# A four-layer graph network on one core: y of layer 2 by rows, layer 1's degrees a batch ahead, and a batch of layer 3 that ends in halves

## The chip, the core and the metric

The kernel runs on one core of a Trainium2 chip. The metric is the device time of one execution in microseconds (us), lower is better. A core has five engines that run side by side, each with a queue of its own: TensorE (PE; its weight loads are listed as PEld), VectorE (DVE), ScalarE (ACT), GpSimd (POOL) and SyncE (SP). SP and POOL issue the transfers (DMAs) here; the data is moved by 16 DMA engines that all queues share. TensorE writes its results to PSUM, all other data on the core lies in SBUF.

## The reference

Sixteen graphs (B = 16) of 1024 nodes (N) with 128 features (D = 128) go through four layers; after each, x is replaced by a layernorm of x + layer(x).

```python
x = _layernorm(x + _L0_gnn_ref(x, adj, ...), axis=-1)            # attention, gated
x = _layernorm(x + _L1_gnn_ref(x, adj, nodemask, ...), axis=-1)  # three SAGE steps
x = _layernorm(x + _L2_gnn_ref(x, adj, ...), axis=-1)            # attention, three gates
x = _layernorm(x + _L3_gnn_ref(x, adj, ...), axis=-1)            # three graph convolutions
```

Layer 1 first thins out the adjacency matrix row by row, then runs three SAGE steps on the thinned matrix, and joins their results by one linear map:

```python
deg = jnp.clip(jnp.sum(adj, axis=-1, keepdims=True), 1.0, None)
agg = jnp.einsum('bij,bjd->bid', adj, x) / deg
out = agg @ Wr + x @ Wx + b
nrm = jnp.maximum(jnp.linalg.norm(out, axis=-1, keepdims=True), NORM_EPS)
return out / nrm * mf[..., None]
...
h1 = _bn(jax.nn.relu(_sage(x, adj_d, Wr1, Wx1, b1, mf)), g1, be1)     # h2, h3 likewise
xc = jnp.concatenate([h1, h2, h3], axis=-1) * mf[..., None]
return (xc @ Wl + bl) * mf[..., None]
```

Here mf is the node mask as a float. The last line is what the code calls y.

## The kernel before

`fast_kernel` runs the four layers in stages over the 16 batches. A second, general kernel stands behind a flag that is computed at the end; in these executions it is skipped. The stages, in time: layer 0 to about 610 us; the thinning to about 990 us; the three SAGE steps (`Step`, l = 0, 1, 2) to about 1636 us; layers 2 and 3 together to the end.

**Order of work.** Each batch's work in a stage is a Python generator that writes instructions and stops at each `yield`. `take_turns` (L811) resumes a list of generators one after the other until all are done. `in_rounds` (L815) does the same with due times: `yield 5` means not to be resumed for five rounds. What is written thus is a program order. From it, a planner sets at build time the order on each engine: the earliest written instruction that is ready by the planner's own estimate of durations goes next. So an instruction can stand in its queue well ahead of its written place, as a filler, where the planner saw an engine without other work. On the chip every queue is then taken in that fixed order. Tiles come from pools with a number of slots per name (`bufs`); a new tile of the name waits until an old one is released. On a queue, an instruction that waits holds all behind it.

**SAGE step 0** (L1510 to L1525). For the i-th batch in `order` (8 to 15, then 0 to 7) the list of generators is: `load` of batch i + 2 (A and x), `first` of batch i + 1, `out` of batch i, `keep` of batch i - 1. `first` (L1392) computes the degrees of its batch: 32 small matmuls of A with a block of twos (`degree_product`, L1276), four copies on ACT to a row on one partition (L1397), a transfer from there to eight partitions, issued by POOL (d<-row, L1399), a minimum, a scaling and a reciprocal on DVE (L1400 to L1403), a transfer to DRAM by POOL (L1404), and a load by SP that spreads the result over all partitions (rdeg, L1389). The next turns of `first` transpose x, split x into two halves hi and lo (L1272, L1273; lo has one slot), cast A to 32 bit (the tiles a, L1293 on DVE and L1295 on ACT), and multiply (L1306), scaled by rdeg (L1416). `keep` multiplies A with the new state in the same way. The matrices A of batches 8 to 15 are on chip; those of 0 to 7 are loaded (A<-dil_d, 1 MB each, L1369) into four slots.

**Layers 2 and 3** (L1546 to L1816). Per batch there are four generators: `before` (y, the layernorm of layer 1, the operands of the attention), `attention` (eight tiles), `mix` (the gates, layer 2's end) and `convolve` (layer 3). In one call of `in_rounds`, batch b - 2 convolves, b - 1 mixes, b attends and b + 1 is prepared; a first call prepares batches 0 and 1, and a last one ends batches 13 to 15.

In `before`, y is formed transposed. With the columns' scaling taken into Wl by `take_norms`, three matmuls per half of 512 nodes have the 128x128 matrix Wl fixed and the states hb moving (L766 for b >= 2, L1636 for b < 2, which uses a PSUM tile py of both halves). ACT adds the bias column blcol and writes yT (L1641). Eight transposes turn yT (L759), DVE multiplies by the mask (yn, L1645) and adds to x (L1648), and `normed` (L787) does the layernorm: statistics and ln_nb on DVE, the power -1/2 on POOL (ln_rstd, L745), the scaling on ACT (L801). `scaled_parts` (L1605) has in layer 3 the other form: a block of states fixed, a weight matrix moving.

`normed` takes a list of pieces; with `spans(True)` a batch is done in two halves. `convolve` does so for the last batch alone (`last`), which also stores by SP; the others store by POOL (L1799). After the stage the check flag is made on DVE (L1829 to L1834), and each engine reads it (L1842).

Of the kernel before, what the change touches and what calls it, by code (L numbers as in the profile page):

```python
# [22 lines left out]
P = 128  # L23
# [616 lines left out]
def fast_kernel(ctx: ExitStack, tc: tile.TileContext, t: dict, out: bass.AP, flag: bass.AP):  # L640
# [554 lines left out]
    class Layers23:  # L1195
# [8 lines left out]
        def weights(self, ps_h):  # L1204
            wts = self.wts
            self.Wl = wts.tile([P, 3, P], F32, name="Wl")
            nc.sync.dma_start(self.Wl, nat(t["L1_gnn_Wl"]))
            self.shift = wts.tile([P, 3, P], F32, name="shift")
            self.blcol = column(wts, t["L1_gnn_bl"], "blcol")
            self.W2T = transposed(wts, ps_h, matrix(wts, t["L2_gnn_W_w"], "l2W"), "l2WT", "h")  # L1210
            self.b2 = column(wts, t["L2_gnn_W_b"], "l2b")
            self.As2 = symmetric(wts, ps_h, matrix(wts, t["L2_gnn_A"], "l2A"), "l2As", "h")
            self.gw = wts.tile([P, 2, 32], F32, name="l2gw")
            nc.vector.memset(self.gw, 0.0)
            self.gb = wts.tile([P, 3], F32, name="l2gb")
# [17 lines left out]

        def take_norms(self, psum):

            pc = psum.tile([P, 1], F32, name="pc", tag="h")
            self.scaled(2)
            for l in range(3):
                nc.tensor.matmul(pc, self.shift[:, l, :], bn_ab[l][:, 1:2], start=(l == 0), stop=(l == 2))
            nc.vector.tensor_add(self.blcol, self.blcol, pc)  # L1240

        def load(self, s, b):
            s.hb = []
# [14 lines left out]
    with ExitStack() as ph:  # L1258
# [56 lines left out]
        class Step:  # L1315
# [73 lines left out]
                nc.sync.dma_start(st.rdeg, bass.AP(tensor=rdeg_d[b].tensor, offset=rdeg_d[b].offset,  # L1389
                                                   ap=[[0, P], [1, N]]))  # L1390

            def first(self, b):  # L1392

                st = self.batches[b]
                row = work.tile([1, N], F16, name="row", bufs=1)
                for acc, c in degree_product(st.A):
                    nc.scalar.copy(row[:, c], acc)  # L1397
                d16 = small.tile([NT, P], F16, name="d16", bufs=1)
                nc.gpsimd.dma_start(d16, row)  # L1399
                nc.vector.tensor_reduce(nodeg[:NT, b:b + 1], d16, AX.X, OP.min)  # L1400
                d8 = small.tile([NT, P], F32, name="d8", bufs=1)
                nc.vector.tensor_scalar(d8, d16, 0.5, 1.0, op0=OP.mult, op1=OP.max)
                nc.vector.reciprocal(d8, d8)  # L1403
                nc.gpsimd.dma_start(rdeg_d[b], d8)  # L1404
                self.load_rdeg(b)
                yield
                st.hT = work.tile([P, N], F32, name="hT")
                for p, c, _ in turned(ps_h, st.x):
                    nc.scalar.copy(st.hT[:, c], p)
                yield  # L1410
                parts = split(st.x)
                pieces = list(widened(st.A))
# [82 lines left out]
        for l in range(3):  # L1495
            step = Step(l, before)
            if l:
                before.norm()
                step.take_norm()
            if l == 2:  # L1500
                order = [b for pair in zip(order[:B // 2], order[B // 2:]) for b in pair]
            if l == 2:
                take_turns(left)
                left = []
            lead = 0 if l == 1 else 1
            take_turns([step.load(b) for b in order[:1 + lead]])
            if l == 0:
                take_turns([step.first(order[0])])
            outs = [step.out(b) for b in order]
            for i in range(B + lag[l]):  # L1510
                streams, left = left, []
                if i + 1 + lead < B:
                    streams.append(step.load(order[i + 1 + lead]))
                if l == 0 and i + 1 < B:
                    streams.append(step.first(order[i + 1]))
                kept = [step.keep(order[i - 1 - lag[l]])] if i > lag[l] else []
                if l == 2:
                    streams += kept
                if i < B:
                    streams.append(outs[i] if l < 2 else islice(outs[i], 2))  # L1520
                if l == 2 and i:
                    streams.append(outs[i - 1])
                if l < 2:
                    streams += kept
                take_turns(streams)  # L1525
                if l == 2 and i == 0:

                    wide_ctx.close()
                    l2 = Layers23()
                elif l == 2 and i == B - 4:  # L1530
# [15 lines left out]
    with ExitStack() as ph:  # L1546
# [4 lines left out]

        ps_w = ph.enter_context(tc.tile_pool(name="l2_pw", bufs=2, space=PSUM, reuse_waits="tile"))

        W2T, b2, As2, gw, gb, nbig, blcol, Wl = l2.W2T, l2.b2, l2.As2, l2.gw, l2.gb, l2.nbig, l2.blcol, l2.Wl
        (U0, U1, U2), (c0, c1, c2) = l2.U, l2.c
        l2.take_norms(ps_h)

# [65 lines left out]
        def before(s, b):  # L1623
# [1 line left out]
            if b:  # L1625
                l2.load(s, b)
            yield 2
            yT = wide("yT")
            if b < 2:

                p = ps_w.tile([P, N], F32, name="py", tag="w")
                cs = [slice(h * 512, (h + 1) * 512) for h in range(H2)]
                for ls in ((0, 1), (2,)):
                    for c in cs:
                        for l in ls:
                            nc.tensor.matmul(p[:, c], Wl[:, l, :], s.hb[l][:, c], start=(l == 0), stop=(l == 2))  # L1636
                turns = [(p[:, c], c) for c in cs]
            else:
                turns = products(ps_h, *((Wl[:, l, :], s.hb[l]) for l in range(3)))
            for p, c in turns:  # L1640
                nc.scalar.activation(yT[:, c], p, AF.Identity, bias=blcol)  # L1641
            yield 1
            yn = rows("yn", 1)
            for p, c, k in turned(ps_h, yT):
                nc.vector.tensor_mul(yn[:, k, :], tiles3(p), half_rows(mf[:, b * NT + k.start:b * NT + k.stop]))  # L1645

            for k in spans(b < 2):
                nc.vector.tensor_add(s.xn[:, k, :], s.xn[:, k, :], yn[:, k, :])  # L1648
            normed(small, s.xn, b < 2)
            yield 5  # L1650
            s.xT = wide("xT", 2)
            for p, c, _ in turned(ps_h, s.xn):
                nc.scalar.copy(s.xT[:, c], p)
# [92 lines left out]

        def convolve(s, b):

            last = b == B - 1
            at = Place(last)  # L1750
            diag = bass.AP(tensor=s.A8.tensor, offset=s.A8.offset, ap=[list(s.A8.ap[0]), [N + P, NT], [1, P]])
            nc.vector.tensor_tensor(diag, diag, identb[:, None, :].to_broadcast([P, NT, P]), op=OP.add, saturate=False)
# [32 lines left out]
            r = at.of("prop", at.x)  # L1785
            for piece in propagated(at, r, parts, A, dB):
                yield 1
            for k in spans(last):
                c = slice(k.start * P, k.stop * P)
                nc.scalar.activation(r[:, c], r[:, c], AF.Identity, bias=c2)  # L1790
            yield 2 if last else 5
            for p, c, k in turned(at.psum, r, at.ptag):
                nc.vector.tensor_add(s.xn[:, k, :], s.xn[:, k, :], tiles3(p))
                if last:
                    normed(small, s.xn, pieces=[k])
            if not last:
                normed(small, s.xn)
            for k in spans(last):
                (nc.sync if last else nc.gpsimd).dma_start(nat(out[b])[:, k, :], s.xn[:, k, :])  # L1799
            yield  # L1800

        state = l2.state
# [63 lines left out]
```

## Time and profile before

| what | value |
|---|---|
| median of three runs | 2682.58 us (2681.59 to 2685.39) |
| the profiled execution: its own time | 2682.24 us |
| its span, first to last instruction | 2680.4 us |
| mean granted TensorE clock | 0.982 |
| busy: PE, DVE, ACT, POOL | 2521.3, 2102.6, 1969.3, 330.8 us |
| weight loads (PEld) | 1800.2 us |
| chain that ended last, by engine | PE 52%, DVE 19%, ACT 11%, POOL 4%, DMA 3% |
| d<-row (L1399), issue to landing, min/median/max | 1.5/1.6/4.7 us |
| A<-dil_d in step 0 and 1, the same | 4.7/4.8/8.6 us |

How to read the lines of the profile. A line of a group or timeline gives the start (us from the span's start), the length, engine, line of the code, operation, the tile written and the tiles read, the shapes, and how many instructions (x) were merged. The bracket at its end says how long the engine had been idle, and what it then got. A line of the chain of waits gives start, length, engine and line: it is followed back from the last instruction, at each step to what released it. In the table of 40 slices each digit is the busy share of one slice in tenths. Matmuls overlap: the time from one to the next in a group is shorter than the length of one.

### The profile page before, as it was taken

To read this page: it belongs to the slowest core of one execution; us is meant where nothing else is said; L and a number is where in the kernel's file an instruction comes from. 1 tells how busy PE (TensorE), PEld (TensorE's weight loads), DVE (VectorE), ACT (ScalarE), POOL (GpSimd) and SP (SyncE) were. 2 spreads that over 40 slices of the span, in tenths; PEclk is the share of its full clock that TensorE was granted. 3 is DMA by queue.
4 is the path that set the end of the run, shared out by engine and by line. 5 is a ranking of instruction groups with operands and counts; after the bars stand their busy time and mean duration, and the time that the engine had idled before them with its cause. 6 is when DMAs were issued, how large, how long until landed. Compare 5 with 4: busy or idle time off the path is not lost.

```text
span 2680.4 us, 44092 instructions
## 1 busy us (share of the span) xinstructions
PE 2521.3 (94%) x16136; PEld 1800.2 (67%) x16136; DVE 2102.6 (78%) x5830; ACT 1969.3 (73%) x3172; POOL 330.8 (12%) x300
## 2 busy tenths in 40 slices
PE   7999999997889879999999998999999999999986
PEld 5667777765666658887788895466666666666655
DVE  6888888987898867777778875777878787887885
ACT  7898889886888776666555534777777777777773
POOL 0001111103000002111122232001101000001010
PEclk9999999998999989999999998999999999999998
DMA  5555545520000052233366672112221111111100
GB/s 193 181 176 171 173 161 174 179 96 21 2 3 2 1 221 90 100 111 134 133 241 236 211 283 111 40 38 73 74 91 64 64 63 63 63 63 63 48 24 26
DMA packets 109187, 285.59 MB, mean 107 GB/s; under 512 B 12192, under 2 KB 52128, under 8 KB 101792
## 3 DMA queue, kind: packets, MB, share of 16 engines
q1 hardware_dynamic: 87776, 196.58, 21.7%
q0 software_dynamic: 21184, 86.09, 8.8%
q8 instruction: 129, 2.11, 0.3%
q14 instruction: 98, 0.80, 0.1%
HBM read 202.78 MB, written 79.82 MB: 105 GB/s over the span
## 4 chain that ended last, share of the span: by engine, by line
PE 52%; DVE 19%; ACT 11%; issue 8%; POOL 4%; DMA 3%; POOLq 0%; ACTq 0%; DVEq 0%; SPq 0%
PE ph L1618 8%; PE acc L1678 7%; PE acc L1306 7%; PE ph L766 6%; PE ph L1432 4%; PE ph L759 3%; PE pmm L1690 3%; PE acc L973 2%; PE pmm L724 2%; ACT em L985 2%; PE ph L1605 2%; ACT xn L801 2%; DVE mid L1096 2%; DVE keep L1147 2%; POOL ln_rstd L745 2%
## 5 line engine op out<-in xcount | busy, mean ns | idle before, releaser
L973 PEld LDWEIGHTS acc<-hs,em 128*128 128x128 f32 x2048 | 248.7, 192 | 37.9 <-issue 26.8
L973 PE MATMUL acc<-hs,em 128*128 128x128 f32 x2048 | 269.1, 279 | 0.7 <-DVE hs L989 0.3
L1678 PE MATMUL acc<-ex,hs 128*128 128x512 f32 x512 | 248.9, 596 | 7.4 <-DVE hs L1705 4.5
L724 PE MATMUL pmm<-xT,G 128*128 128x512 f32 x512 | 251.4, 604 | 1.4 <-DVE mx L983 0.7
L801 ACT ACTIVATE xn<-xn,ln_nb,ln_rstd 128x128 f32<-128x128 f32 x512 | 204.7, 480 | 55.9 <-DVE ln_nb L799 55.8
L1306 PE MATMUL acc<-a,hi 128*128 128x512 f32 x768 | 233.6, 398 | 11.1 <-DVE a L1293 8.0
L1306 PE MATMUL acc<-a,lo 128*128 128x512 f32 x768 | 229.6, 393 | 5.8 <-DVE lo L1273 5.8
L745 POOL TENSOR_TENSOR ln_rstd<-ln_rstd,mhalf 128x8 f32<-128x8 f32 (+1 forms) x68 | 108.3, 1593 | 969.2 <-DVE ln_rstd L742 513.4
L983 DVE CUSTOM_DVE_ANT_0 em<-pmm,msk 128x1024 f32<-128x1024 f32 x128 | 155.9, 1218 | 35.1 <-PE pmm L724 32.8
L985 ACT ACTIVATE em<-em,mx 128x1024 f32<-128x1024 f32 x128 | 146.0, 1141 | 48.2 <-DVE mx L983 46.5
L1698 ACT ACTIVATE ex<-em,mn 128x1024 f32<-128x1024 f32 x128 | 146.9, 1147 | 45.0 <-DVE mn L1695 44.0
L1690 PE MATMUL pmm<-G,hT 128*128 128x512 f32 (+3 forms) x416 | 175.3, 523 | 0.1
L1695 DVE CUSTOM_DVE_ANT_0 em<-pmm,msk 128x1024 f32<-128x1024 f32 x128 | 155.4, 1214 | 24.5 <-PE pmm L1692 22.3
L1306 PEld LDWEIGHTS acc<-a,hi 128*128 128x128 f32 x768 | 142.2, 189 | 42.4 <-DVE a L1293 10.6
L1306 PEld LDWEIGHTS acc<-a,lo 128*128 128x128 f32 x768 | 143.5, 189 | 40.2 <-DVE lo L1273 10.5
L1156 ACT ACTIVATE carry<-pc,negone 128x1024 fp8e4<-128x1024 f32 x128 | 141.3, 1115 | 26.7 <-PE pc L1155 23.8
L931 ACT ACTIVATE carry<-an 128x1024 fp8e4<-128x1024 f32 x128 | 134.1, 1049 | 23.9 <-DMA an<-in_adj 23.3
L980 ACT ACTIVATE msk<-carry,l0nbig 128x1024 bf16<-128x1024 fp8e4 x128 | 145.9, 1140 | 0.0
L1686 ACT ACTIVATE msk<-A,nbig 128x1024 bf16<-128x1024 fp8e4 x128 | 144.3, 1138 | 0.0
L1618 PE MATMUL ph<-A,hi 128*128 128x512 f32 x512 | 143.2, 420 | 0.8 <-DVE zn L1607 0.6
L1678 PEld LDWEIGHTS acc<-ex,hs 128*128 128x128 f32 x512 | 88.6, 190 | 76.8 <-issue 54.7
L1295 ACT CAST a<-A 128x1024 fp32r<-128x1024 fp8e4 x96 | 98.4, 1048 | 54.5 <-PE acc L1306 53.4
(317 smaller groups left out, 6186.6 us busy)
## 6 DMA issues: line engine op xcount, KB each, us to landing
an<-in_adj SPq DMA_DIRECT2D x128, 512.0 KB, 4.1
adj_d<-carry POOLq DMA_DIRECT2D x16, 1024.0 KB, 4.6
A<-dil_d SPq DMA_DIRECT2D x16, 1024.0 KB, 5.6
rdeg<-rdeg_d SPq DMA_DIRECT2D x32, 512.0 KB, 3.8
A<-adj_d SPq DMA_DIRECT2D x16, 1024.0 KB, 4.8
ag_d<-ag POOLq DMA_DIRECT2D x24, 512.0 KB, 5.4
ag<-ag_d SPq DMA_DIRECT2D x24, 512.0 KB, 5.5
x_d<-xn POOLq DMA_DIRECT2D x16, 512.0 KB, 3.9
```

The lines of the kernel that those rows point to most:

```text
L724: nc.tensor.matmul(p[:, h * 512:(h + 1) * 512], lhsT, rhs[:, h * 512:(h + 1) * 512], start=True, stop=True)
L745: nc.gpsimd.tensor_tensor(r, r, mhalf[:, :n], op=OP.pow)
L766: nc.tensor.matmul(p, W, x[:, c], start=(i == 0), stop=(i == len(pairs) - 1))
L801: nc.scalar.activation(r[:, k.start + i, :], r[:, k.start + i, :], AF.Identity, scale=rstd[:, i:i + 1], bias=nb[:, i:i + 1])
L973: nc.tensor.matmul(s.acc[:, c], em[:, c], hs, start=(jt == 0 and k % 4 == 0), stop=(jt == NT - 1 and k % 4 == 3))
L983: nc.vector.tensor_tensor_reduce(em, e, msk, 1.0, 3.0e38, op0=OP.add, op1=OP.min, accum_out=mn)
L985: nc.scalar.activation(em, em, AF.Exp, scale=-1.0, bias=mn, accum_out=sm)
L1306: nc.tensor.matmul(acc, part[:, jt, :], pieces[h * NT // 2 + k][:, jt - 2 * k, :], start=(part is parts[0] and jt == 0), stop=(part is par ...
L1618: nc.tensor.matmul(p, part[:, jt, :], A[jt][:, c], start=(jt == 0 and i == 0), stop=(jt == NT - 1 and i == 1))
L1678: nc.tensor.matmul(s.acc[:, c], hs, ex[:, c], start=(jt == 0), stop=(jt == NT - 1))
L1690: nc.tensor.matmul(e[:, c], s.hT[:, js], s.G[:, c], start=True, stop=True)
L1695: nc.vector.tensor_tensor_reduce(row, e, msk, 1.0, 0.0, op0=OP.add, op1=OP.min, accum_out=mn)
```

## The change

Three edits, made together.

1. **y by rows.** The bias is loaded as a row over all partitions, blrow, into the slot of the raw matrix l2A (so after that one's last use); `take_norms` adds to it a 128x128 product in place of a column. In `before`, POOL multiplies mask and bias row to a tile yb (128x1024). Then for each block of 128 nodes the three states' blocks are the fixed operand and Wl the moving one, so that the sum comes out with nodes on the partitions: 24 matmuls of 128 columns in place of 6 of 512. yT, its two activations and the eight transposes are gone; DVE adds yb where it multiplied by the mask. The layernorm comes two rounds after the sums in place of one, and the next step six rounds later in place of five.
2. **Degrees a batch ahead.** The degree work is a generator of its own, `degrees`, written last in the list, for batch i + 2 in iteration i, with its product in the third turn. The load of rdeg stays in `first`. The first two batches' degrees are done ahead of the loop.
3. **Ends in halves.** Batch 14 (`near`) of layer 3 ends as batch 15 does: bias, turn, addition and layernorm by halves, stores by SP, and two rounds' pause in place of five.

```diff
-            self.blcol = column(wts, t["L1_gnn_bl"], "blcol")
...
+            self.blrow = row_bcast(wts, t["L1_gnn_bl"], P, "l2A")
...
-            pc = psum.tile([P, 1], F32, name="pc", tag="h")
+            pc = psum.tile([P, P], F32, name="pc", tag="h")
             self.scaled(2)
             for l in range(3):
-                nc.tensor.matmul(pc, self.shift[:, l, :], bn_ab[l][:, 1:2], start=(l == 0), stop=(l == 2))
-            nc.vector.tensor_add(self.blcol, self.blcol, pc)
+                nc.tensor.matmul(pc, bn_ab[l][:, 1:2].to_broadcast([P, P]), self.shift[:, l, :], start=(l == 0), stop=(l == 2))
+            nc.vector.tensor_add(self.blrow, self.blrow, pc)
...
-            def first(self, b):
+            def degrees(self, b):
 
                 st = self.batches[b]
+                yield
+                yield
                 row = work.tile([1, N], F16, name="row", bufs=1)
                 for acc, c in degree_product(st.A):
                     nc.scalar.copy(row[:, c], acc)
                 d16 = small.tile([NT, P], F16, name="d16", bufs=1)
                 nc.gpsimd.dma_start(d16, row)
+                yield
                 nc.vector.tensor_reduce(nodeg[:NT, b:b + 1], d16, AX.X, OP.min)
...
                 nc.gpsimd.dma_start(rdeg_d[b], d8)
+                yield
+
+            def first(self, b):
+
+                st = self.batches[b]
                 self.load_rdeg(b)
...
-                take_turns([step.first(order[0])])
+                take_turns([chain(step.degrees(order[0]), step.first(order[0])), step.degrees(order[1])])
...
+                if l == 0 and i + 2 < B:
+                    streams.append(step.degrees(order[i + 2]))
...
-            yT = wide("yT")
+            yb = rows("yT")
+            nc.gpsimd.tensor_tensor(yb, per_row(mf[:, b * NT:(b + 1) * NT]), per_col(blrow), op=OP.mult)
+
+            def summed(p, blocks, ls):
+                for i, j in enumerate(blocks):
+                    for l in ls:
+                        nc.tensor.matmul(p[:, i * P:(i + 1) * P], s.hb[l][:, j * P:(j + 1) * P], Wl[:, l, :],
+                                         start=(l == 0 and (i % 4 == 0 or len(ls) == 3)), stop=(l == 2 and (i % 4 == 3 or len(ls) == 3)))
+
             if b < 2:
                 p = ps_w.tile([P, N], F32, name="py", tag="w")
...
                 for ls in ((0, 1), (2,)):
...
+                    summed(p, range(NT), ls)
+                turns = [(p[:, h * 512:(h + 1) * 512], range(4 * h, 4 * h + 4)) for h in range(H2)]
             else:
-                turns = products(ps_h, *((Wl[:, l, :], s.hb[l]) for l in range(3)))
-            for p, c in turns:
-                nc.scalar.activation(yT[:, c], p, AF.Identity, bias=blcol)
-            yield 1
+                turns = ((p, blocks) for p, _, blocks in halves(ps_h))
             yn = rows("yn", 1)
-            for p, c, k in turned(ps_h, yT):
-                nc.vector.tensor_mul(yn[:, k, :], tiles3(p), half_rows(mf[:, b * NT + k.start:b * NT + k.stop]))
+            for p, blocks in turns:
+                if b >= 2:
+                    summed(p, blocks, range(3))
+                k = slice(blocks[0], blocks[-1] + 1)
+                nc.vector.tensor_add(yn[:, k, :], tiles3(p), yb[:, k, :])
+            yield 2
...
-            yield 5
+            yield 6
...
-            last = b == B - 1
+            last, near = b == B - 1, b >= B - 2
...
-            for k in spans(last):
+            for k in spans(near):
                 c = slice(k.start * P, k.stop * P)
                 nc.scalar.activation(r[:, c], r[:, c], AF.Identity, bias=c2)
-            yield 2 if last else 5
+            yield 2 if last else 2 if near else 5
...
-                if last:
+                if near:
                     normed(small, s.xn, pieces=[k])
-            if not last:
+            if not near:
                 normed(small, s.xn)
-            for k in spans(last):
-                (nc.sync if last else nc.gpsimd).dma_start(nat(out[b])[:, k, :], s.xn[:, k, :])
+            for k in spans(near):
+                (nc.sync if near else nc.gpsimd).dma_start(nat(out[b])[:, k, :], s.xn[:, k, :])
```

More of the change, by code (lines that the diff above doesn't have):

```diff
@@ L1552, in fast_kernel @@
         ps_w = ph.enter_context(tc.tile_pool(name="l2_pw", bufs=2, space=PSUM, reuse_waits="tile"))
-        W2T, b2, As2, gw, gb, nbig, blcol, Wl = l2.W2T, l2.b2, l2.As2, l2.gw, l2.gb, l2.nbig, l2.blcol, l2.Wl
+        W2T, b2, As2, gw, gb, nbig, blrow, Wl = l2.W2T, l2.b2, l2.As2, l2.gw, l2.gb, l2.nbig, l2.blrow, l2.Wl
         (U0, U1, U2), (c0, c1, c2) = l2.U, l2.c
@@ L1627, in before @@
             yield 2
-            yT = wide("yT")
+            yb = rows("yT")
[5 more added lines that the diff above has]
+                                         start=(l == 0 and (i % 4 == 0 or len(ls) == 3)), stop=(l == 2 and (i % 4 == 3 or len(ls) == 3)))
             if b < 2:
                 p = ps_w.tile([P, N], F32, name="py", tag="w")
-                cs = [slice(h * 512, (h + 1) * 512) for h in range(H2)]
                 for ls in ((0, 1), (2,)):
[L1634 to L1637, printed above, removed]
-            else:
-                turns = products(ps_h, *((Wl[:, l, :], s.hb[l]) for l in range(3)))
-            for p, c in turns:
-                nc.scalar.activation(yT[:, c], p, AF.Identity, bias=blcol)
-            yield 1
+                    summed(p, range(NT), ls)
+                turns = [(p[:, h * 512:(h + 1) * 512], range(4 * h, 4 * h + 4)) for h in range(H2)]
+            else:
+                turns = ((p, blocks) for p, _, blocks in halves(ps_h))
             yn = rows("yn", 1)
-            for p, c, k in turned(ps_h, yT):
-                nc.vector.tensor_mul(yn[:, k, :], tiles3(p), half_rows(mf[:, b * NT + k.start:b * NT + k.stop]))
+            for p, blocks in turns:
[4 more added lines that the diff above has]
+            yield 2
             for k in spans(b < 2):
```

## The prediction

> **What bounds the kernel now.** I read the busy shares in 40 slices first, then the busy time of each engine by stretches, then the chain of waits and the timeline of the three places that the change touches.
>
> ```profile
> PE   7999999997889879999999998999999999999986
> DVE  6888888987898867777778875777878787887885
> POOL 0001111103000002111122232001101000001010
> ```
>
> Each digit is a slice of 67 us. TensorE is at nine tenths wherever the change works: slices 15 to 19 (the first SAGE layer, "layer 1, step 0" in the code) and 25 to 38 (layers 2 and 3). So a microsecond counts there if it leaves TensorE's queue, or if TensorE now waits for it. The stretches are finer:
>
> ```profile
> 1083.40:1105.00 21.60, 21.39 (x145) 17.75 (x145) 16.50 (x28) 14.62 (x21) 4.29 (x5) 1.00 0.28 98
> 1264.84:1288.49 23.65, 21.82 (x147) 17.75 (x146) 16.57 (x28) 14.70 (x20) 4.20 (x5) 1.00 0.39 134
> 2320.00:2382.00 62.00, 61.69 (x269) 38.77 (x268) 49.11 (x142) 47.71 (x86) 5.95 (x4) 1.00 0.20 68
> 2600.00:2620.00 20.00, 10.85 (x31) 4.63 (x29) 15.03 (x57) 15.09 (x32) 3.93 (x3) 0.75 0.04 13
> ```
>
> The columns are length, then busy time of PE, weight loads, DVE, ACT and POOL. Row 1 is an early batch of step 0: TensorE idles 0.2 us. Row 2 is a late one: 1.8 us. Row 3 is the steady part of layers 2 and 3: TensorE idles 0.3 of 62, with 13 us to spare on DVE and 14 on ACT. Row 4 is the tail, where nothing is full.
>
> **What the Trainium skill says.** (1) "TensorE: Matmul & The Clock Gate", specification table and Part 2: the next weights load under a running matmul, and the vector engines and GpSimd take their queues strictly in order. The trace agrees: weight loads of 0.190 us (f32) stand in groups that advance every 0.111 us (L1605, 0.89 us for 8). (2) "GPSIMD Engine Reference", section 3.1: a two-input elementwise operation takes about 2.6 cycles per element, 4.5 us for 2048. For 1024 I estimate 2.2 us. The trace has no such operation. (3) "DMA: Bandwidth & Descriptors", "Issuing engines are not separate DMA queues": all transfers share 16 engines and interleave. The trace agrees: d<-row lands in 1.6 us (median), and in 4.7 us beside the 1 MB load of A.
>
> **Part 1, y by rows.** Written matmuls appear twice in the trace in f32 (168 L766 rows on hb,Wl for 14 batches, 6 written each).
>
> ```profile
> 2371.26 2.58 PE ph L766 x6
> 2373.84 0.89 PE ph L1605 x8
> ...
> 2499.71 0.44 PE ph L759 x4
> ```
>
> These are lines of the chain of waits. The first is half of the old y: 2.58 us for 6 of 512 columns, 0.43 each. The second is the form that the new y takes, a 128-column block fixed and a 128x128 matrix moving: 0.111 each. The third is half of the turn. Per batch it removes 12 x 0.43 = 5.16 and 8 x 0.11 = 0.88, and adds 48 x 0.111 = 5.34: -0.70 us of TensorE. Batches 2 to 15 lie in the full stretch: 14 x 0.70 = **-9.8**. ACT loses 2 x 0.67 us, DVE keeps its two 0.68 us reads of PSUM (an addition where it was a product): both have slack, so nothing. POOL gains the product of mask and bias. Bounds: 1.2 us (DVE's row of that size, L1648) and the estimate of 2.2, which I take; the only POOL elementwise row, a power, is far dearer (1.64 us for 8 columns). It needs only the slot of the last batch's rows, so it can run a batch early on a POOL that is busy 6 us in 62, but a layernorm's power queued behind it would wait; that is rival C. Sharing SBUF ports could slow DVE by at most those 2.2 us of its 13 spare.
>
> At the **start** of layer 2 nothing hides latency. Now the second half of batch 0 is turned behind the products of batch 1, which wait for a load (TensorE resumes at 1645.71), so its yn comes at 1650.52; batch 1's follow at 1653.04 after ACT at 1650.67 and eight transposes. In the new form, the bias row exists at about 1641.2 (blcol at 1640.92, plus 0.28), the POOL product at 1643.5, and both halves of batch 0 follow. Batch 1's sums end near 1651.0 (48 x 0.111 from 1645.71), its yn starts at once: 1.7 us before 1653.04, with batch 0's DVE work out of the way. I take **-2**, between +1 (a POOL product of twice the price) and -4. The row's load waits for the slot of l2A (last read at 1615.0, SP then idle until 1639.9): nothing.
>
> **Part 2, degrees one batch ahead.** The late batches of step 0:
>
> ```profile
> 1194.17 0.51 POOL L1399 DMA_DIRECT2D d<-row  x1 [6.55 <-ACT row L1397]
> 1198.85 0.27 DVE L1400 TENSOR_REDUCE nodeg<-d 8x1 f32<-8x128 f16 x1 [2.43 <-DMA d<-row]
> 1202.70 1.20 PE L1306 MATMUL acc<-a,hi 128*128 128x512 f32 x4 [1.30 <-DVE a L1293]
> 1207.46 0.73 PE L1281 MATMUL acc<-A,step 128*32 128x256 fp8e4 x20
> 1208.69 0.73 PE L1306 MATMUL acc<-a,lo 128*128 128x512 f32 x2 [0.50 <-DVE lo L1273]
> ```
>
> SP issues the load of A at 1193.85, the degree row leaves 0.3 us later and takes 4.7 us; DVE stands in nodeg for 2.43 us, the casts and lo queued behind it come late, and TensorE idles 1.30 and 0.50. Six batches do this (nodeg waits 14.8 us in 6 times). Groups of L1281 x20 stand at 1184.19 and 1301.83, five batches apart: 23.53 each, against 21.68 before. So 6 x 1.85 = 11.1 us is at stake. The change issues the same 32 small matmuls, 4 ACT copies (0.36 each), the POOL issue (0.51), three DVE operations (0.27, 0.20, 0.92), and the POOL store (0.50), a batch earlier and in the third turn rather than the first; on POOL this passes the hT store, the power and the ag store. By then A has landed (4.8 us after its issue), so the row should need 1.6 us again, and what is late next is TensorE itself at 21.68. The 20 matmuls at 1207.46 fill 0.65 us that TensorE would spend waiting for lo; that A is there in time (loads at 1193.85, 1217.41, one batch ahead of the written place), so I expect another batch's matmuls in the same hole. If none come: 14 x 0.65 = +9. The second product in the prologue falls where TensorE waits 2.60 us for hi; it takes 1.0 us off the path at 1003.72, and its ACT copies (1.47) may stand ahead of that hi: I set these against each other. I keep 1 us of the 11.1 for the DVE work in its new place: **-10**, between -12 and 0 (the wait goes along), or +9.
>
> **Part 3, second-to-last batch in halves.** It ends last:
>
> ```profile
> 2662.39 1.13 ACT L1790 ACTIVATE prop<-prop,c 128x1024 f32<-128x1024 f32 x1
> 2665.47 1.64 DVE L794 BATCH_NORM_STATS2 ln_st<-xn 128x6 f32<-128x128 f32 x8
> 2670.05 3.18 ACT L801 ACTIVATE xn<-xn,ln_nb,ln_rstd 128x128 f32<-128x128 f32 x8 [6.53 <-DVE ln_nb L799]
> 2673.53 0.93 POOL L1799 DMA_DIRECT2D out<-xn  x1 [3.72 <-ACT xn L801]
> ```
>
> Halved, the bias of the first half can run at about 2659.7 (its prop at 2658.72 plus 0.66), and the second half's at 2662.5, behind the last batch's normalisation on ACT. From there: bias 0.72, turn 0.7, addition 0.68, statistics 0.86 + 0.36, power 1.02 (the 4-column row), ln_nb 0.16, ACT 1.65: 2668.7 with small gaps 2669, against 2673.2. The store from SP lands in 2.2 us (last batch) against 4.6. But the check flag also ends the program: at 2671.20, then 4.0 us of a TensorE branch; it follows DVE, whose last ln_nb moves from 2669.84 to about 2667.3. So the end moves by that 2.5, not by 4.5: **-2.5**, between -1 and -5.
>
> **Sum.** -9.8 - 2 - 10 - 2.5 = -24.3. The profiled execution took 2682.24 us (span 2680.4), 0.34 below the median of three: 2657.9, so 2658.
>
> **Rivals.** A, as summed: 2658, own range 2649 to 2664. Chance 0.62. B, the degrees keep their wait or lose their hole: part 2 gives between 0 and +9 less the other 14.3, so 2668 to 2677, most of it near 2668. For it: DVE is in order, and where nodeg is put follows an estimate that knew nothing of the slow row. Against it: no large load is under way where the third turn lies. Chance 0.16. C, slower: POOL's product stands just ahead of a layernorm's power in every round. ln_nb then holds DVE's queue for up to 2.2 us, the scalings hs behind it hold TensorE (it already waits 0.29 us for hs at 2489.51). Price 14 x 2.2 = +31 on -24.3: 2689. It turns the sign from 24.3/14 = 1.7 us a round. For: three powers a round, nothing in the trace shows this product's price. Against: the product is ready a batch early. Chance 0.09. D, the new form of y doesn't pay: above 0.126 us a matmul (6.04/48) part 1 gives nothing in the steady part and the time is 2668 or more, up to 2677. For: 0.190 us weight loads. Against: L1605 at 0.111 between other work. Chance 0.08. E, gains and losses cancel, 2677 to 2688: 0.05.
>
> **Numbers.** 0.2% (5.4 us) is about what a measurement of this kernel can tell from none. Faster: A, B, D, 0.86; same: E, 0.05; slower: C, 0.09. The range from 2648 to 2672 takes all of A, most of B and part of D, about 0.8.
>
> **What would show it.** Part 1: per round of layers 2 and 3 61.63 us becomes 60.9, with no L759 on yT; POOL's product near 2.2 us. Part 2: no nodeg wait above 0.5 us, the late batches at 21.7. Part 3: out from SP near 2669. The prediction is wrong if ln_nb <- POOL grows in the rounds, if lo holds TensorE 0.8 us a batch, or if the new y advances slower than 0.12 us.

## The result, and the profile after

The kernel after takes 2660.16 us (median of 6 runs, 2656.06 to 2665.67), the kernel before 2682.09 beside it (6 runs, 2678.87 to 2685.39): a ratio of 0.9918, 95% interval 0.9906 to 0.9930, or 22 us less (19 to 25). The profiled execution took 2657.81 us, its span is 2656.1. The forecast was 2658, with a range of 2648 to 2672. The time is right; the terms that make it up are not, and the sections below are about that.

Five places can be found in both traces, each the start of one named instruction on VectorE or GpSimd. Times are us from the start of the span; the last column is what the prediction had for the stretch that ends there.

| place | before | after | ahead by | gained in the stretch | forecast |
|---|---|---|---|---|---|
| first power rn of step 0 | 1011.62 | 1012.05 | -0.4 | | |
| first power rn of step 1 (part 2 lies before it) | 1362.58 | 1346.13 | 16.5 | 16.9 | 10 |
| last power rn of step 2 | 1631.59 | 1614.67 | 16.9 | 0.5 | 0 |
| gate gt of batch 1 (the start of layer 2) | 1768.96 | 1750.88 | 18.1 | 1.2 | 2 |
| gate gt of batch 13 (12 rounds) | 2508.33 | 2487.28 | 21.1 | 3.0 | 8.4 to 9.8 |
| end of the span (part 3) | 2680.4 | 2656.1 | 24.3 | 3.2 | 2.5 |

In this execution part 2 gave two thirds more than forecast, part 1 about a third of its 11.8. The errors cancel, by luck.

The stretches of the kernel after, with the columns of the prediction's table (length, then busy time of PE, weight loads, DVE, ACT, POOL, then granted clock, DMA share, GB/s):

```profile
1090.73:1112.09 21.36, 21.35 (x146) 17.98 (x145) 16.50 (x27) 14.98 (x21) 3.84 (x6) 1.00 0.28 99
1240.86:1262.21 21.35, 21.34 (x146) 17.96 (x145) 16.50 (x27) 14.97 (x21) 3.84 (x5) 1.00 0.46 147
2303.45:2365.45 62.00, 61.59 (x297) 41.02 (x295) 49.34 (x142) 47.58 (x88) 7.84 (x5) 1.00 0.19 68
2579.00:2599.00 20.00, 11.55 (x30) 5.04 (x29) 15.03 (x57) 15.09 (x32) 3.93 (x3) 0.78 0.03 10
```

The late batch of step 0 (row 2) is now as long as the early one (row 1), and TensorE has no idle time in either. In row 3 TensorE still idles 0.4 of 62 us: the new y has not made room there, it has only changed what TensorE is busy with. POOL shows the product: 7.84 us in place of 5.95.

Where the degree work went, in a late batch of step 0 (timeline of the kernel after; the bracket is idle time of the engine before it, and what ended it):

```profile
1199.73 1.06 PE L1281 MATMUL acc<-A,step 128*32 128x256 fp8e4 x32
1200.84 1.49 ACT L1399 CAST row<-acc 1x256 f16<-1x256 f32 x4 [0.35 <-PE acc L1281]
1202.63 0.56 POOL L1401 DMA_DIRECT2D d<-row  x1 [2.81 <-ACT row L1399]
1204.40 0.27 DVE L1403 TENSOR_REDUCE nodeg<-d 8x1 f32<-8x128 f16 x1
1205.86 0.60 PE L1440 MATMUL ph<-Wx,hT 128*128 128x128 f32 x4
1206.31 0.93 PE L759 MATMUL ph<-identf,n 128*128 128x128 f32 x7
1206.99 0.70 PE L1306 MATMUL acc<-a,lo 128*128 128x512 f32 x2
```

The 1 MB load of A, issued at 1195.55, landed at 1201.39; the row leaves at 1202.63 and lands 1.59 us later (1.6 forecast). The 32 small matmuls are one block now, in the place where TensorE had waited 1.30 us for the casts of A. nodeg has no bracket: the row has landed. The gap ahead of lo, which I had expected another batch's degree matmuls to fill, is filled by four products and the transposes of `out`, and lo has no bracket either.

### The profile page after: what moved, and what is told of

It reads as the page before. It is cut to its first block, busy times and chain, and to the rows that moved or that the text cites. A ratio compares the mean times of both kernels' runs of the same rounds, so it can differ in the third digit from the quotient of the medians.

```text
span 2656.1 us, 44982 instructions
## 1 busy us (share of the span) xinstructions
PE 2509.0 (94%) x16580; PEld 1838.7 (69%) x16584; DVE 2106.4 (79%) x5832; ACT 1957.0 (74%) x3141; POOL 356.3 (13%) x316
## 3 DMA queue, kind: packets, MB, share of 16 engines
q8 instruction: 133, 2.18, 0.3%
## 4 chain that ended last, share of the span: by engine, by line
PE 53%; DVE 19%; ACT 13%; issue 5%; POOL 4%; DMA 2%; POOLq 0%; ACTq 0%; DVEq 0%; SPq 0%
PE acc L1306 9%; PE ph L1628 8%; PE acc L1694 6%; PE ph L1440 5%; PE ph L759 3%; PE ph L1644 3%; PE acc L973 2%; PE pmm L1706 2%; PE pmm L724 2%; PE ph L1615 2%; ACT em L985 2%; PE ph L766 2%; ACT xn L801 2%; DVE mid L1096 2%; DVE keep L1147 2%
## 5 line engine op out<-in xcount | busy, mean ns | idle before, releaser
L1156 ACT ACTIVATE carry<-pc,negone 128x1024 fp8e4<-128x1024 f32 x128 | 141.4, 1116 | 27.0 <-PE pc L1155 24.3
L1295 ACT CAST a<-carry 128x1024 fp32r<-128x1024 fp8e4 x96 | 98.9, 1047 | 43.4 <-PE acc L1306 43.2
```

## Experiments

Each is one edit of the kernel before or after. Ratios are to the kernel before, run beside it on the same chip, with the 95% interval; "ahead" is against the kernel before, taken from the places above. Ahead of the first place, in stages that no edit touches, single executions differ by up to 5 us; so a stretch is always taken from place to place. The planner makes the order anew for each kernel, so a run shows an edit together with the order that comes of it.

### One part at a time

Each is the kernel before with one of the three edits of the change.

> Part 1 alone (y by rows), the rest as before. Theory S (the places where the two traces part company belong to the parts that lie there: up to the first product of layer 2 the kernel after is 16.8 us ahead, over the rounds it gains 4.2 us, at the end 3.3): 2682 - 4 = 2678, 0.25 us gained per round (61.57 to 61.32), nothing gained at the start of layer 2. Theory P (the sizes of the prediction are right and the parts disturb each other when made together): 2682 - 11.8 = 2670, with rounds of 60.9.

> Part 2 alone (degrees one batch ahead). Theory S: -16.5, so 2665.5; the late batches of step 0 at 21.36 us each in place of 23.56, and the early ones at 21.36 in place of 21.68, but for one or two in which the degree row lands late. Theory P: -10, so 2672, with the late batches at 21.7.

> Part 3 alone (second-to-last batch of layer 3 in halves). Theory S: -3.3, so 2679: the flag comes 1.5 us earlier after the last long run of products, and 1.8 us more is gained between the flag and the end. Theory P: -2.5, all of it ahead of the flag.

| edit | ratio | by place |
|---|---|---|
| y by rows alone | 0.9998 (0.9989 to 1.0007) | start 1.3, twelve rounds 2.3, to the flag nothing more, flag to end 1.3 lost |
| degrees alone | 0.9941 (0.9927 to 0.9954) | step 0: 15.5; from there to the end within 0.8 of that |
| halves alone | 0.9993 (0.9984 to 1.0001) | last power of step 2 to the end: 2.1 |

By place, theory S holds: the stretches belong to the parts, and the parts hardly disturb each other. Part 2 is most of the change's gain. By time, part 1 can't be told from no change (0.5 us, between -1.9 and 3.0, where S had 4 and P 11.8), and part 3 hardly; what can be said of them comes from one trace each. How far one trace carries, two stretches show: y by rows loses 1.3 us from flag to end, and the degrees alone gain 1.4 at the start of layer 2, both in stages that these edits leave alone.

### What part 2's gain rests on

```diff
             def degrees(self, b):
                 st = self.batches[b]
-                yield
-                yield
                 row = work.tile([1, N], F16, name="row", bufs=1)
```

> The kernel after with the degrees one batch ahead, but in the first turn in place of the third. Theory W (what is gained in the late batches of step 0 is that the degree row is no longer under way beside the 1 MB load of A): the row leaves beside that load again and takes 4.5 us, VectorE waits for it, and the late batches are back at 23 to 23.6 us each, 10 to 13 us of the gain lost: 2670 to 2673. Theory H (what is gained is being a batch ahead, so that no one needs the degrees soon): the late batches stay at 21.4 and the time at 2660 to 2662.

The ratio is 0.9994 (0.9985 to 1.0002): all is lost. But not as either theory had it. The row did leave beside the load of A and took 4.3 to 6.0 us, yet VectorE waited for it only twice (3.2 us in all): being a batch ahead hides a slow row. And every batch became 22.95 us long, the early ones too, which load no A. One of these early batches (timeline):

```profile
1113.23 1.48 ACT L1397 CAST row<-acc 1x256 f16<-1x256 f32 x4
1114.53 0.17 DVE L744 TENSOR_SCALAR rn<-ss 128x8 f32<-128x8 f32 x1
1115.00 0.51 POOL L1399 DMA_DIRECT2D d<-row  x1 [1.58 <-ACT row L1397]
1115.53 1.68 POOL L745 TENSOR_TENSOR rn<-rn,mhalf 128x8 f32<-128x8 f32 x1
1117.23 0.17 DVE L1457 TENSOR_TENSOR rn<-rn,mf 128x8 f32<-128x8 f32 x1 [2.53 <-POOL rn L745]
1119.46 1.20 PE L1306 MATMUL acc<-a,hi 128*128 128x512 f32 x4 [1.35 <-DVE a L1293]
```

rn is ready for its power at 1114.70, but GpSimd stands in the issue of d<-row, which waits for ScalarE's four copies. The power starts 0.8 us late, and VectorE, which takes its queue in order, idles 2.53 us with the cast of A behind it. TensorE then waits 1.35. In the kernel after the issue comes behind the power. So the third turn is needed, to keep GpSimd's queue free for the power; being a batch ahead hides a row that is slow. Whether the third turn would do without being a batch ahead, no run shows.

### The product of mask and bias

```diff
-            nc.gpsimd.tensor_tensor(yb, per_row(mf[:, b * NT:(b + 1) * NT]), per_col(blrow), op=OP.mult)
+            nc.vector.tensor_tensor(yb, per_row(mf[:, b * NT:(b + 1) * NT]), per_col(blrow), op=OP.mult)
```

> The kernel after, with the product of mask and bias on VectorE in place of GpSimd. Theory K (GpSimd's product and VectorE's additions of two tiles in SBUF hold each other up: the two additions at the start of layer 2 take 1.45 us each in place of 0.69 while GpSimd's product runs): the start gains about 1 to 3 us, since each product costs VectorE 1.2 us and spares it 1.5. Theory R (what the rounds lose against the prediction, 0.45 us each, is also GpSimd holding up VectorE): rounds fall from 61.33 to about 60.9, 4 to 5 us in all. Theory O (the rounds' loss is the new order of the instructions on TensorE and has nothing to do with GpSimd): rounds stay at 61.3, the sum is 0 to -3.

The ratio is 0.9950 (0.9936 to 0.9963): about 10 us dearer than with GpSimd. The start came 1.8 us earlier than after's (theory K), but the rounds grew from 61.37 to 62.48 us. Of the 1.22 us that the product takes on VectorE, 1.1 show up in the round, though VectorE is idle 12 us of it. TensorE's waits over the rounds (us in all, times, longest), first those of the kernel after, then those of this one:

```profile
PE acc L1694 <- DVE hs L1721: 3.5, 12, 0.3
```

```profile
PE ph L759 <- ACT prop L1806: 4.9, 11, 0.5
PE acc L1694 <- DVE hs L1721: 3.7, 12, 0.3
PE ph L766 <- ACT x3T L1777: 1.5, 10, 0.2
```

The new waits name ScalarE, and ScalarE gets its inputs late from VectorE: over the rounds it waits 42.2 us for ln_nb (19.0 in the kernel after) and 32.5 for gt (20.4), though only 37.9 for mn (68.7). That VectorE's queue is the way from the product to the round is read from these waits. Neither theory R nor O foresaw this.

The next one leaves the product out: the bias row is added as it is.

```diff
-            yb = rows("yT")
-            nc.gpsimd.tensor_tensor(yb, per_row(mf[:, b * NT:(b + 1) * NT]), per_col(blrow), op=OP.mult)
...
-                nc.vector.tensor_add(yn[:, k, :], tiles3(p), yb[:, k, :])
+                nc.vector.tensor_add(yn[:, k, :], tiles3(p), per_col(blrow)[:, k, :])
```

> The kernel after without the product of mask and bias: the bias row is added as it is, so the mask is left out of the bias. Theory K (GpSimd's product blocks additions of two SBUF tiles on VectorE): the start of layer 2 gains what the two blocked pairs of additions lost, 1.7 us each, of which the second lies on the path, 2 to 3.5 us in all; rounds unchanged at 61.3. Theory R (GpSimd's product also costs the rounds their 0.45 us): rounds of 60.9, 5 us more. Theory O: rounds stay at 61.2 to 61.4.

The ratio is 0.9911 (0.9896 to 0.9926); rounds of 61.37, the same as with the product. Theory R falls: in the rounds GpSimd's product costs nothing. The start came 3.0 us earlier, measured from the last power of step 2 to the gate of batch 1, as theory K said. The start of layer 2 in the kernel after shows the blocking that K supposes:

```profile
1627.78 2.98 DVE L1664 TENSOR_TENSOR xn<-xn,yn 128x512 f32<-128x512 f32 x2
1628.01 2.21 POOL L1639 TENSOR_TENSOR yT<-mf,l2A 128x1024 f32<-128x1024 f32 x1 [1.91 <-DVE yn L1660]
1636.45 2.98 DVE L1664 TENSOR_TENSOR xn<-xn,yn 128x512 f32<-128x512 f32 x2
1636.67 2.21 POOL L1639 TENSOR_TENSOR yT<-mf,l2A 128x1024 f32<-128x1024 f32 x1 [1.54 <-DVE yn L1660]
```

The slot of yb comes free when yn is done; so GpSimd's next product starts just when VectorE adds yn to xn, and the two additions take 2.98 us in place of 1.29. The Trainium skill ("SBUF — State Buffer", "Who interferes with whom") says that an operation of VectorE with two SBUF inputs and one of GpSimd that reads SBUF exclude each other for a whole instruction. The trace agrees: 1.69 us lost beside a product that takes 2.2, and 1.9 where it runs alone. In the steady rounds GpSimd's product falls beside two operations of VectorE that read PSUM, and these kept their 0.69 us; the one with two SBUF inputs that starts in its last 0.2 us (lo, L1620) takes 0.74 in place of 0.68.

That the blocking is there is shown; how much of the start it costs is not. The kernel with pauses 1 and 6 (below) keeps both products and both pairs of 3.0 us, and yet has the gate of batch 1 3.2 us earlier than the kernel after. So the order behind the additions weighs as much as the additions themselves.

Two edits try to win the start back:

```diff
-            nc.gpsimd.tensor_tensor(yb, per_row(mf[:, b * NT:(b + 1) * NT]), per_col(blrow), op=OP.mult)
+            (nc.vector if b < 3 else nc.gpsimd).tensor_tensor(yb, per_row(mf[:, b * NT:(b + 1) * NT]), per_col(blrow), op=OP.mult)
```

> The kernel after with the product of the first three batches on VectorE, the others on GpSimd as before. Theory K: the additions at the start take 0.69 us each again; with the whole product on VectorE the first gates of layer 2 came 2.9 us earlier against the last power of the SAGE steps than in the kernel before, with GpSimd 1.3 later: so 4 us gained, 2656. Rival: the start waits for the load of batch 1 in both, and VectorE's own products take what the additions win: 0 to -1.

and, with no product at all for the first three batches,

```diff
...
-                nc.vector.tensor_add(yn[:, k, :], tiles3(p), yb[:, k, :])
+                if b >= 3:
+                    nc.vector.tensor_add(yn[:, k, :], tiles3(p), yb[:, k, :])
+                else:
+                    for i, j in enumerate(blocks):
+                        nc.vector.scalar_tensor_tensor(yn[:, j, :], blrow, mf[:, b * NT + j:b * NT + j + 1], tiles3(p)[:, i, :], op0=OP.mult, op1=OP.add)
```

> The kernel after; for batches 0 to 2 there is no product on GpSimd: VectorE multiplies mask and bias row and adds the sum in one instruction per block of 128 nodes (eight small ones in place of two additions); the other batches as after. Theory K (at the start GpSimd's product blocks VectorE's additions of two SBUF tiles, which without any product gave 3 us by the trace): the two pairs of additions take 1.3 us each again, the first gates of layer 2 come 2 to 3 us earlier against the last power of the SAGE steps, the rounds stay at 61.3: 2657 to 2658. Rival: the eight small instructions cost VectorE more than the additions saved (over 0.4 us each): no gain, 2660 to 2662.

Ratios 0.9904 (0.9889 to 0.9919) and 0.9920 (0.9906 to 0.9933): the kernel after's time within what can be told. In both, each addition takes 0.69 us again. In the first the start gains 0.9 us against after's. In the second eight small instructions take 2.15 us where two additions took 1.29; it is 2.1 us ahead at the gate of batch 1, but its next round is 64.1 us long and gives it all back. The rivals were right on the time. No version here beats the kernel after measurably.

### What the rounds lost

The new pauses looked like bookkeeping, and the prediction priced them at nothing. Three kernels undo them, both or one at a time (pause from y to the layernorm, pause from there to the turn of xn; after: 2 and 6).

```diff
                 nc.vector.tensor_add(yn[:, k, :], tiles3(p), yb[:, k, :])
-            yield 2
+            yield 1
...
-            yield 6
+            yield 5
```

> The kernel after, with the pauses of the kernel before in before(): the layernorm one round after the sums, the next step five rounds later, so that the turn of xn is written two rounds earlier. Theory O (the rounds' loss against the prediction is order: xT and hT now stand on ScalarE among the two tanh of mix, and the products of ehi wait 0.55 us a round for a PSUM tile that hT reads late): the wait goes, rounds fall from 61.33 to about 60.9, the time from 2660 to 2654 or 2655. Theory N (the new pauses are needed since the sums end later; without them TensorE waits for the layernorm): rounds of 61.5 or more, 2663 or more.

> The kernel after, with five rounds in place of six between layernorm and the turn of xn; the layernorm stays two rounds after the sums. Theory L (the old pauses cost 1.3 us a round since the layernorm's statistics stand ahead of the attention's minimum on VectorE): only the other pause matters, rounds stay at 61.3 or fall to 60.9 when the products of ehi no longer wait for hT; time 2654 to 2661. Theory M (what matters is when xT and hT come): rounds of 62 or more, 2668 or more.

> The kernel after, with the layernorm one round after the sums in place of two, and six rounds after it. Theory L: rounds of 62.5 or more as with both old pauses (63.0), time 2672 to 2683. Theory M: rounds of 61 to 61.5, 2656 to 2662.

| pauses | ratio | mean round, batches 1 to 13 |
|---|---|---|
| 2 and 6 (after) | 0.9918 (0.9906 to 0.9930) | 61.37 |
| 1 and 5 | 0.9995 (0.9986 to 1.0003) | 62.81 |
| 2 and 5 | 0.9919 (0.9905 to 0.9932) | 61.45 |
| 1 and 6 | 0.9961 (0.9947 to 0.9974) | 62.33 |
| kernel before (1, 1 and 5) | 1 | 61.61 |

With the old pauses the whole change is worth nothing. By its numbers theory N was right, and then L: the layernorm's pause decides (62.33 is a little under what L said), the other matters less (0.1 us a round where that one is 2, 0.5 where it is 1). With pauses 1 and 5 (timeline):

```profile
2125.47 1.64 DVE L794 BATCH_NORM_STATS2 ln_st<-xn 128x6 f32<-128x128 f32 x8
2127.03 0.63 DVE L796 BATCH_NORM_AGGREGATE ln_mv<-ln_st 128x2 f32<-128x6 f32 x8
2127.57 1.19 DVE L1711 CUSTOM_DVE_ANT_0 em<-pmm,msk 128x1024 f32<-128x1024 f32 x1
2128.86 1.16 ACT L1714 ACTIVATE ex<-em,mn 128x1024 f32<-128x1024 f32 x1 [4.83 <-DVE ln_rstd L742]
2132.25 0.28 DVE L1721 TENSOR_SCALAR hs<-hn,rs 128x128 f32<-128x128 f32 x1
2132.67 1.52 PE L1694 MATMUL acc<-ex,hs 128*128 128x512 f32 x3 [0.51 <-DVE hs L1721]
```

and in the kernel after:

```profile
2234.52 1.21 DVE L1711 CUSTOM_DVE_ANT_0 em<-pmm,msk 128x1024 f32<-128x1024 f32 x1
2237.53 0.28 DVE L794 BATCH_NORM_STATS2 ln_st<-xn 128x6 f32<-128x128 f32 x1
2237.80 0.27 DVE L794 BATCH_NORM_STATS2 ln_st<-xn 128x6 f32<-128x128 f32 x1
2237.99 0.27 DVE L1721 TENSOR_SCALAR hs<-hn,rs 128x128 f32<-128x128 f32 x1
2238.17 1.24 DVE L794 BATCH_NORM_STATS2 ln_st<-xn 128x6 f32<-128x128 f32 x6
```

In the first the statistics stand as a block of 2.2 us ahead of the attention's minimum em; ScalarE idles 4.83 us until the minimum comes (the bracket names ln_rstd, but ex reads em, which ends 0.1 us before ex starts), the scaling hs follows late, and TensorE waits for it. In the second the minimum and hs go ahead, and the statistics fill what is left.

Theory O, on what the rounds still lose, fell with the second of the three: xT came a round earlier and the round stayed the same. Where the loss sits can be shown. For eight rounds I took TensorE's time from the start of each matmul to the start of the next and counted what exceeds the time of the fastest tenth of that form, a form being the same line, tiles and shape (us per round; work is the rest). The totals change by about 1 us with how the forms are grouped, the differences between the kernels by about 0.1:

```
                               before    after   pauses 2, 5
round                          61.57     61.33     61.31
work                           59.08     58.35     58.38
excess                          2.50      2.98      2.93
  into the products of ehi      0        0.28      0
  among the products of ehi     0.01     0.28      0.23
  into the turn of hT           0.19     0         0.33
  among acc <- ex,hs            0.11     0.25      0.21
```

The work fell by 0.73 us, as forecast (0.70). Another 0.48 came up as longer steps between matmuls: 0.55 more around the products of ehi and 0.14 among acc <- ex,hs, 0.19 less at the turn of hT. With pauses 2 and 5 the step into the products of ehi is gone and one into the turn of hT is there instead, so moving xT moves these steps rather than ending them. What holds those products up in the new order I could not settle.

### The end

```diff
-                (nc.sync if near else nc.gpsimd).dma_start(nat(out[b])[:, k, :], s.xn[:, k, :])
+                (nc.sync if last else nc.gpsimd).dma_start(nat(out[b])[:, k, :], s.xn[:, k, :])
```

> The kernel after with the two stores of the second-to-last batch on GpSimd in place of SyncE, the halves kept. Theory E (of part 3's 3.3 us, what lies between flag and end, 1.8 us, belongs to the stores from SyncE): flag as after, flag to end 9.0 to 9.5 us in place of 7.4, the time 1.5 to 2 us above the kernel after. Theory F (the end follows the flag alone, and the 1.8 us come from elsewhere): flag to end stays at 7.4 to 7.7.

The ratio is 0.9917 (0.9903 to 0.9930), not to be told from after's. By its trace, flag to end is 8.8 us, against 7.4 in the kernel after and 9.2 before. That points to theory E: of the 1.8 us gained there, some 1.4 would be SyncE's. It is not settled, since the stretch scatters: over all traces it is 6.9 to 7.9 us in nine with stores from SyncE, 8.8 in a tenth (pauses 1 and 6), and 8.8 to 10.4 in the four with the last store from GpSimd.

## Why the prediction was right, and where it wasn't

**The time was right because two terms missed in opposite directions**: part 2 by 6.9 us in the profiled execution, part 1 by about 7.6. That they are of about one size is luck: nothing in the sum ties the one to the other.

**Part 2** ("what is late next is TensorE itself at 21.68"). The mechanism was right, and rival B falls: nodeg's wait of 2.43 us a batch is gone and the late batches run like the early ones (two waits of 1.5 and 0.6 us are left, in early batches). The floor was wrong. The 21.68 us of the early batches held 0.21 us of waiting for lo and 1.17 for the degree matmuls, which take 0.99 in one block; with the gap ahead of lo filled by `out`, a batch takes 21.36. The late six gained 14.2 in place of 11.1, the prologue 1.8, and the last two iterations 1.1; the early ones gained nothing, since two rows landed late (last section). I took 1 us off for VectorE's work in its new place; that was unfounded. The profile caught a good execution, too: from the first place to step 1, nine other profiles with the same step 0 gained 12.3 to 15.6 us where after's gained 16.9. This is much of why the median (22 us gained) lies behind the profile (24.3).

**Part 1, rounds** ("14 x 0.70 = -9.8"). The price of the form was right: 5.55 us for 48 matmuls, 0.116 each, where 0.111 was forecast, in place of 6.22 for the old form; rival D falls. The step that failed is the next: that work taken from a TensorE that is busy 61.7 us of 62 comes off the time. Its busy time held steps longer than their form needs, which no view lists as idle, and the new order has 0.48 us more of them. The round fell by 0.25. Why these steps are longer stays open.

**Part 1, the moved layernorm.** The prediction named the pauses nowhere in its sum. They carry 1 to 1.4 us a round. The change had them right, so the forecast was spared; as a step of the argument it was missing, and "13 us to spare on DVE" was no argument for it: 1.22 us more on VectorE cost 1.1.

**Part 1, start** ("I take -2"). It gained 1.2, and even that is no more than the scatter: the kernel with the degrees alone gained 1.4 there. yn of batch 1 came 0.9 us earlier against the last power of step 2 (the prediction had 1.7, though its own two times, 1651.0 and 1653.04, lie 2.0 apart), but the two additions after it lost 1.7 to GpSimd. I had named shared ports and bounded their cost by slack, which holds in a full round and not at a start where "nothing hides latency".

**Part 3** ("-2.5"): 3.2, and not by the path of the sum. The flag moved by 1.5 us where 2.5 was forecast. The sum had the second half's statistics right behind its addition; in the kernel after they stand on VectorE behind the first half's ln_nb, which waits for GpSimd's power:

```profile
2642.75 0.69 DVE L1809 TENSOR_TENSOR xn<-xn,ph 128x512 f32<-128x512 f32 x1 [0.66 <-PE ph L759]
2643.66 1.01 POOL L745 TENSOR_TENSOR ln_rstd<-ln_rstd,mhalf 128x4 f32<-128x4 f32 x1 [4.15 <-DVE ln_rstd L742]
2644.70 0.16 DVE L799 SCALAR_TENSOR_TENSOR ln_nb<-ln_mv,ln_rstd 128x4 f32<-128x4 f32 x1 [0.86 <-POOL ln_rstd L745]
2644.78 0.86 DVE L794 BATCH_NORM_STATS2 ln_st<-xn 128x6 f32<-128x128 f32 x4
```

The addition ends at 2643.44, the statistics start 1.3 us later. The other 1.8 us gained lie between flag and end, which the prediction had held constant. Its "store from SP lands in 2.2 us" failed: 4.7 (last section).

**Rival C**: the product took 1.89 us in the rounds (2.2 forecast). VectorE's waits for a layernorm's power did grow, which the prediction had named as a sign of being wrong: from 4.8 to 6.2 us in two rounds, the longest from 1.1 to 1.4. But without the product the longest is 1.4 too, the waits over the twelve rounds are the same (32.5 us, with it 32.4), and so are the rounds. The product is not what makes them grow.

## What to carry to other kernels

When an engine is busy 99% of a stretch, cost a removed instruction at its full price only if the order around it stays; here two thirds of what it saved came back as longer steps between other matmuls, and one pause was worth more than the edit. Spare time on VectorE was not room for an instruction (12 us idle a round, and 1.22 us more of work cost 1.1): ask what stands behind it at that spot. A transfer's issue is an instruction of its queue too: with it behind the power a batch took 21.4 us, with it ahead 22.95.

## Not expected of the hardware

**Slow degree rows stand beside loads of instructions.** In the kernel after two degree rows landed in 3.4 and 2.4 us with no other transfer of the program under way. The DMA view of the first (of a queue: packets, MB, share of the 16 engines' time; of an issue: KB, us to landing):

```profile
q8 instruction: 1, 0.02, 2.0%
q0 software_dynamic: 32, 0.00, 0.6%
d<-row POOLq DMA_DIRECT2D x1, 2.0 KB, 3.4
```

Beside the 32 packets of the row there is one of 16 KB of the queue that loads instructions, 1.27 us long by its record; the row's last two packets start as it ends. VectorE waited 1.5 us, lo behind it, and the batch took 22.9 us in place of 21.4. The second row met a packet of 8 KB. In the nine other profiles with this step 0 a late batch met one as well (rows of 3.1 to 3.6 us), and in all ten together each of the 28 rows over 2.2 us has such a packet beside it, with the row's last two packets starting as it ends (a 29th row like these took 2.18 us). In 19 other rows the packet had ended 0.3 us or more before the row's own packets moved, and these landed in 1.6 to 2.1 us. So it is the overlap that goes with the delay; no run took the loads away. The Trainium skill ("Runtime: NRT & Kernel Launch", "Instruction fetch mechanics") says that blocks of 16 KiB are fetched while the current one executes and that the cost of crossing into the next is mostly hidden. That is said of the engine that fetches; what stands in these traces is a cost to another transfer.

**The last store of the program is slow on any queue.** The last but one store of after landed in 2.3 us, the last, of the same size, in 4.7; before, the last took 4.1 from GpSimd. Its DMA view in the kernel after:

```profile
q1 hardware_dynamic: 528, 0.26, 20.5%
q14 instruction: 8, 0.07, 4.5%
q8 instruction: 1, 0.02, 2.6%
out<-xn SPq DMA_DIRECT2D x1, 256.0 KB, 4.7
```

The view has nine loads of instructions, seven of which start before the store has landed, at the time of the branch on the flag. In all fourteen traces the last store (4.0 to 5.1 us) has 5 to 9 such loads beside it, and the one before it (2.2 to 2.8 us) none. That they slow it is inferred from this overlap; no run took them away.
